# A GRU and an expert-choice FFN on one core: the loads and masks of the kernel's head are dealt out anew over three queues

## The chip, the cores and the metric

The kernel runs on 1 core of a Trainium2 chip. The time is device microseconds of one execution, the median of several; the profile is one further execution, recorded by the hardware profiler. A core has TensorE (PE; its weight loads are PEld), VectorE (DVE), ScalarE (ACT), GpSimd (POOL) and SyncE (SP). SP, ScalarE and GpSimd can each issue transfers (DMA), which 16 DMA engines carry out.

## The reference

```python
x: (16, 256, 512)   cond_2048: (16, 512)   # float32
# GRU over 256 steps, state h: (16, 512), first state cond_2048
gi = x_t @ W_ih + b_ih;  gh = h @ W_hh + b_hh          # 3 gates of 512 each
r = sigmoid(i_r + h_r);  z = sigmoid(i_z + h_z);  n = tanh(i_n + r * h_n)
h = (1 - z) * n + z * h                                 # the states are xf: (4096, 512)
# FFN: each of 16 experts takes its 256 best rows
S = softmax(xf @ router_w + router_b);  G, idx = top_k(S.T, 256)
y = zeros.at[idx].add(G[..., None] * (xf[idx] @ expert_w + expert_b))
out = x + y
```

All 16 experts share one matrix `expert_w`, so each row's product is the same for every expert that takes it.

## The kernel before, in words

Everything is float32 and stays in the core's memory: W_ih as `wih` and W_hh as `whh` (3 MB each, laid out as 128 partitions x 4 blocks x 3 gates x 512), x as `xs` (32 groups of 8 steps, 128 partitions x 512 each) and the states as `ht`. The 256 steps run one after the other. Step s adds h times `whh` into PSUM (`h_part`, L409, gates r, n, z in this order), ScalarE and VectorE make the new state from that (L465 to L505), and the next step needs it. The products of x with `wih` (`x_part`, L396) are made for two steps at a time and fill TensorE between. For that, a group of x is also loaded in another layout (`xa`, eight pieces of 32 KB, `load_xa`, L236) and turned by VectorE (`turn_x`, L252). `xa` has one buffer, which group 1 takes over after group 0.

Behind the steps follow the choice of the rows (a binary search over the scores), the expert's products that are still missing, and the output. The 0/1 matrices `ident`, `same_f`, `same_h`, `before_f` and `row_of` are used there alone, and are made at the very start by GpSimd and VectorE (L86 to L106) with scratch tiles in a pool of their own, `masks`. That pool is closed again before the weights' tiles are opened, so `wih` and its neighbours get the same room.

The head of the kernel, up to step 0, is what the change touches:
- GpSimd's queue: `zero` (L86, which TensorE's first operations read), the masks' operations, `c0` set to zero (L208), then four loads of biases (L266) and four of cond (L268).
- SP's and ScalarE's queues, each half of every weight load: wih's gate r, the eight pieces of x's group 0 (four each), wih's gates n and z, whh's gates r, n and z (`load_rows`, L228). SP goes on with group 1's `xa`, `expert_w`, `router_w` and two biases (L281 to L285).
- TensorE: PSUM cleared (L112), the biases added by matmuls (L300), then `x_part` for steps 0 to 3 (gates r and n first, then z), then step 0.
- VectorE: the masks' operations, x's group 0 turned, cond turned (L314), the biases copied out of PSUM (L309 to L311), the first state `hs` (L319), then step 0.

The order within SP's and ScalarE's queues of the head is written out by hand (`manual_schedule`, L272); for the others a scheduler sets the order there. In the recurrence it is written out for all engines. Loads from SP and ScalarE share eight semaphores in turn, and so do those from GpSimd with eight others: a load that takes over a semaphore waits in its queue until the load that had it has landed. Biases and cond are loaded into rooms of `xs` (groups 26 to 31) that x fills much later: `load_x` (L245) loads four pieces of group g during the steps of group g.

Of the kernel before, what the change touches and what calls it, by code (L numbers as in the profile page):

```python
# [8 lines left out]
F32 = mybir.dt.float32  # L9
BF16 = mybir.dt.bfloat16  # L10
F16 = mybir.dt.float16
I32 = mybir.dt.int32
# [6 lines left out]
def kernel(  # L19
# [34 lines left out]
    nc = tc.nc  # L54
    B, T, D = x.shape
    E = router_w.shape[1]
    P = 128
    QD = 32
    KC = D // P
    TG = P // B  # L60
    NG = T // TG
# [4 lines left out]
    xs = const.tile([P, NG, D], F32, name="xs")  # L66
# [11 lines left out]
    GH = P // E  # L78
    ident = const.tile([P, P], F32, name="ident")
# [4 lines left out]
    ones_b = const.tile([P, B], F32, name="ones_b")  # L84
    zero = const.tile([P, QD], BF16, name="zero")
    nc.gpsimd.memset(zero, 0.0)  # L86
    make_identity(nc, ident)
    nc.gpsimd.memset(ones_b, 1.0)
    with tc.tile_pool(name="masks", bufs=1) as mk:
        shift = GH.bit_length() - 1  # L90
        at = mk.tile([P, 3], I32, name="at")
        nc.gpsimd.iota(at[:, 0:1], pattern=[[0, 1]], base=0, channel_multiplier=1)
        nc.vector.tensor_single_scalar(at[:, 1:2], at[:, 0:1], shift, ALU.logical_shift_right)
        nc.vector.tensor_single_scalar(at[:, 2:3], at[:, 0:1], GH - 1, ALU.bitwise_and)
        at_f = mk.tile([P, 3], F32, name="at_f")
        nc.vector.tensor_copy(at_f, at)
        to_i = mk.tile([P, 2, E, GH], I32, name="to_i")
        nc.gpsimd.iota(to_i[:, 0, :, :], pattern=[[1, E], [0, GH]], base=0, channel_multiplier=0)
        nc.gpsimd.iota(to_i[:, 1, :, :], pattern=[[0, E], [1, GH]], base=0, channel_multiplier=0)
        to = mk.tile([P, 2, P], F32, name="to")  # L100
        nc.vector.tensor_copy(to, to_i.rearrange("p o e h -> p o (e h)"))
        nc.vector.tensor_scalar(same_f, to[:, 0, :], at_f[:, 1:2], None, ALU.is_equal)
        nc.vector.tensor_copy(same_h, same_f)
        nc.vector.tensor_scalar(before_f, to[:, 1, :], at_f[:, 2:3], None, ALU.is_gt)
        nc.vector.tensor_tensor(before_f, before_f, same_f, ALU.mult)
        nc.vector.tensor_scalar(row_of, to[:, 1, 0:GH], at_f[:, 2:3], None, ALU.is_equal)  # L106
# [77 lines left out]
    with (  # L184
# [17 lines left out]
        b_raw = xs[0:2, NG - 4 : NG - 1, :]  # L202
        b_n = xs[0:1, NG - 1, :]
        b_r = xs[0:1, NG - 6, 0:E]
        c0 = xs[:, NG - 5, 0:P]
        ones = wts.tile([2, QD], F32, name="ones")
        nc.vector.memset(ones, 1.0)
        nc.gpsimd.memset(c0, 0.0)  # L208

# [7 lines left out]
        def columns(ap, j):  # L219

            return ap.rearrange("p (c j i) -> p j c i", j=KC, i=QD)[:, j]

        def load_rows(dst, src, form):

            rows = src.rearrange(form, c=KC)
            for h in range(2):
                ks = slice(KC // 2 * h, KC // 2 * (h + 1))
                queues[h].dma_start(out=dst[:, ks, :], in_=rows[:, ks, :])  # L228
# [3 lines left out]
        def load_xa(g, xa, j, qs):  # L232

            for o in range(2):
                q = QD * j + B * o
                qs[o].dma_start(  # L236
                    out=xa[q : q + B],
                    in_=x[:, g * TG + o : (g + 1) * TG : 2, j * P : (j + 1) * P],
                )
# [7 lines left out]
        def new_xa():  # L247
            return xap.tile([P, TG // 2, P], F32, name="xa")

        def turn_x(g, xa):  # L250
            t = xtp.tile([P, TG // 2, P], F32, name="xt")
            nc.vector.transpose(  # L252
                t.rearrange("p q (c r) -> p q c r", c=KC), xa.rearrange("p q (i c) -> p q c i", c=KC)
            )
            xT[g] = t

        queues = (nc.sync, nc.scalar)
        ET = mybir.EngineType
        xa0 = new_xa()
        for dst, src in (  # L260
            (b_raw[0:1], b_ih.rearrange("(o g d) -> o g d", o=1, d=D)),
            (b_raw[1:2], b_hh.rearrange("(o g d) -> o g d", o=1, d=D)),
            (b_n, b_hh[2 * D :].rearrange("(o d) -> o d", o=1)),
            (b_r, router_b.rearrange("(o e) -> o e", o=1)),
        ):
            nc.gpsimd.dma_start(out=dst, in_=src)  # L266
        for j in range(KC):
            nc.gpsimd.dma_start(  # L268
                out=c0[QD * j : QD * j + B, :].rearrange("b (c i) -> b c i", c=KC), in_=columns(cond, j)
            )  # L270
        xa1 = new_xa()
        with tc.manual_schedule(engines={ET.SP, ET.Activation}):  # L272
            for i, gate in enumerate((0, 2, 1)):
                load_rows(wih[:, :, i, :], w_ih[:, gate * D : (gate + 1) * D], "(p c) n -> p c n")
                if i == 0:
                    for j in range(KC):
                        load_xa(0, xa0, j, queues)
            for gate in (0, 2, 1):
                load_rows(whh[:, :, gate, :], w_hh[:, gate * D : (gate + 1) * D], "(c p) n -> p c n")
            for j in range(KC):  # L280
                load_xa(1, xa1, j, (nc.sync, nc.sync))  # L281
            nc.sync.dma_start(out=ewr[:, :, E:], in_=expert_w.rearrange("(c p) n -> p c n", c=KC))
            nc.sync.dma_start(out=ewr[:, :, 0:E], in_=router_w.rearrange("(c p) n -> p c n", c=KC))
            nc.sync.dma_start(out=eb, in_=expert_b.rearrange("(o d) -> o d", o=1).to_broadcast([P, D]))
            nc.sync.dma_start(out=rb, in_=router_b.rearrange("(o e) -> o e", o=1).to_broadcast([P, E]))  # L285
# [131 lines left out]
                    )  # L417

        turn_x(0, xa0)
        xa_next = xa1  # L420
        for z in (False, True):
            for p in range(2):
# [10 lines left out]
        with tc.manual_schedule(engines={ET.PE, ET.Activation, ET.DVE, ET.Pool, ET.SP}):  # L433
            units = []
            for s in range(T):
                p, odd = divmod(s, 2)
                g, c = divmod(s, TG)
# [21 lines left out]
                elif not apart:  # L459
# [12 lines left out]
                t, n, nT, zT = (  # L472
                    [gp.tile([P, P // 2], F32, name=f"{name}{half}") for half in range(2)]
                    for name in ("t", "n", "nT", "zT")
                )
# [50 lines left out]
                elif g + 2 < NG:  # L526
                    if c == KC:
                        xa_next = new_xa()
                    j = c - KC
# [33 lines left out]
    with (  # L563
# [32 lines left out]
        for bit in range(HIGH, -1, -1):  # L596
# [6 lines left out]
            n = counts[:, bit : bit + 1]  # L603
# [63 lines left out]
        for g in [g for g in range(NG) if g not in late_groups] + late_groups:  # L667
            while g in late_groups and g not in late_done:
# [5 lines left out]
                out=out[:, g * TG : (g + 1) * TG, :], in_=xs[:, g, :]  # L674
# [32 lines left out]
```

## Time and profile before

| | |
|---|---|
| runs | 1201.14, 1201.27, 1209.14 us; median 1201.27 |
| the profiled execution | 1205.67 us, span from first to last instruction 1203.9 |
| TensorE busy | 1163.5 us, 97% of the span; weight loads 1052.9 us |
| VectorE, ScalarE, GpSimd busy | 699.1, 323.3, 96.0 us |
| mean granted clock of TensorE | 0.994 |
| GpSimd's last mask operation (L99) | starts at 1.66, takes 0.35 us |
| VectorE's mask operations (L93 to L106) | from 1.24 to 3.33 us |
| first weight load issued (SP and ScalarE, L228) | 3.42 us |
| x of group 0 turned (L252) | starts at 11.81, takes 1.08 us |
| first state (L319) | 13.73 us |
| stretch 40 to 1130 us (the steps) | TensorE busy 1076.7 of 1090 us, clock 1.00, 19 GB/s |

Times in the profile are microseconds from the span's start. Busy shares are tenths of a slice. A bracket behind an instruction says how long its engine sat idle before it, and what ended that idle time. The lists of loads give the number, the size of each and the median time from issue to landing. q1 and q10 are the queues of SP and ScalarE, q0 that of GpSimd.

### The profile page before, as it was taken

What the parts mean: (1) busy time and instruction counts of PE and PEld (TensorE: products, weight loads), DVE (VectorE), ACT (ScalarE), POOL (GpSimd) and SP (SyncE); (2) the same over time, 40 slices, a digit from 0 to 9 for tenths busy, and PEclk for the clock granted to TensorE, in tenths of its full rate; (3) what the DMA queues carried; (4) which work ended last, traced back from release to release, by engine and by line L of the source; (5) the groups of instructions that cost most, each with busy time, mean ns of one, the idle gap of its engine ahead of it and who ended that gap; (6) DMA issues with size and microseconds to landing.
All of it is one profiled execution on the core that took longest, in us unless ns stands there. A gap on an engine that the chain in (4) does not pass through costs nothing. (4 is left out here: it accounts for less than half of the span.)

```text
span 1203.9 us, 80849 instructions
## 1 busy us (share of the span) xinstructions
PE 1163.5 (97%) x36490; PEld 1052.9 (87%) x36490; DVE 699.1 (58%) x3919; ACT 323.3 (27%) x1435; POOL 96.0 (8%) x398
## 2 busy tenths in 40 slices
PE   5999999999999999999999999999999999999897
PEld 3899999999999999989999999999999999998443
DVE  2555655565555655555565555565565556565776
ACT  0222222222222222322222222222222222222220
POOL 2000000000000000000000000000000000000000
PEclk9999999999999999999999999999999999999998
DMA  7200000000000000000000000000000000000008
GB/s 233 63 22 20 20 19 21 19 20 19 20 22 20 19 18 22 20 20 17 22 19 20 19 21 20 20 19 20 22 18 21 18 22 20 20 9 13 2 2 281
DMA packets 48730, 38.06 MB, mean 32 GB/s; under 512 B 7744, under 2 KB 40576, under 8 KB 48384
## 3 DMA queue, kind: packets, MB, share of 16 engines
q1 hardware_dynamic: 46176, 29.56, 8.4%
q8 instruction: 286, 4.69, 1.6%
q10 hardware_dynamic: 1952, 3.28, 0.8%
q14 instruction: 60, 0.49, 0.1%
q0 software_dynamic: 256, 0.05, 0.0%
HBM read 24.47 MB, written 8.39 MB: 27 GB/s over the span
## 5 line engine op out<-in xcount | busy, mean ns | idle before, releaser
L409 PE MATMUL ra<-whh,hs 128*16 128x128 f32 (+1 forms) x8192 | 348.4, 274 | 6.9 <-DVE zT L494 4.9
L409 PE MATMUL hn<-whh,hs 128*16 128x128 f32 (+1 forms) x8192 | 348.1, 273 | 0.8 <-DMA whh<-in_L_cond_W_hh_dram 0.8
L482 DVE TENSOR_TENSOR t<-r,hn 128x64 f32<-128x64 f32 x512 | 90.2, 217 | 369.8 <-PE hn L409 366.8
L396 PE MATMUL ra<-wih,xt 128*32 128x256 f32 x4096 | 288.4, 381 | 5.1 <-DMA wih<-in_L_cond_W_ih_dram 3.2
L409 PE MATMUL zz<-whh,hs 128*16 128x128 f32 (+1 forms) x8192 | 288.2, 273 | 3.0 <-DMA whh<-in_L_cond_W_hh_dram 1.9
L409 PEld LDWEIGHTS hn<-whh,hs 128*16 128x16 f32 (+1 forms) x8192 | 259.7, 104 | 1.2 <-DMA whh<-in_L_cond_W_hh_dram 1.1
L409 PEld LDWEIGHTS ra<-whh,hs 128*16 128x16 f32 (+1 forms) x8192 | 246.3, 103 | 15.5 <-issue 5.9
L409 PEld LDWEIGHTS zz<-whh,hs 128*16 128x16 f32 (+1 forms) x8192 | 240.5, 103 | 6.4 <-issue 3.5
L465 ACT ACTIVATE r<-ra 128x128 f32<-128x128 f32 x256 | 71.1, 278 | 591.3 <-PE ra L409 591.3
L396 PEld LDWEIGHTS ra<-wih,xt 128*32 128x32 f32 x4096 | 158.9, 110 | 38.3 <-issue 11.6
L486 ACT ACTIVATE n<-t 128x64 f32<-128x64 f32 x512 | 103.5, 248 | 192.8 <-DVE t L484 192.6
L396 PE MATMUL zz<-wih,xt 128*32 128x128 f32 x4096 | 146.6, 273 | 1.9 <-issue 1.4
L396 PEld LDWEIGHTS zz<-wih,xt 128*32 128x32 f32 x4096 | 129.0, 110 | 17.1 <-issue 5.0
L491 DVE STREAM_TRANSPOSE nT<-n 128x64 f32<-128x64 f32 x512 | 100.6, 234 | 57.3 <-ACT n L486 57.0
L494 DVE STREAM_TRANSPOSE zT<-zs 128x64 f32<-128x64 f32 x512 | 121.8, 238 | 3.6 <-ACT zs L487 3.0
L505 DVE TENSOR_TENSOR hs<-v,nT 128x32 f32<-128x32 f32 x512 | 101.9, 199 | 21.7
L502 DVE TENSOR_TENSOR v<-u,zT 128x32 f32<-128x32 f32 x512 | 104.4, 204 | 8.9
L363 PE MATMUL pe<-ewr,ht 128*32 128x136 f32 (+1 forms) x1920 | 108.2, 276 | 0.0
L484 DVE TENSOR_TENSOR t<-t,ra 128x64 f32<-128x64 f32 x512 | 88.2, 213 | 0.1
L363 PEld LDWEIGHTS pe<-ewr,ht 128*32 128x32 f32 x1920 | 76.5, 110 | 10.9 <-issue 0.5
L497 DVE TENSOR_TENSOR u<-hs,nT 128x32 f32<-128x32 f32 x512 | 78.3, 153 | 0.0
L136 PE MATMUL pe<-ewr,ht 128*32 128x256 f32 x1088 | 69.5, 395 | 1.9 <-ACT pe L156 1.9
(107 smaller groups left out, 513.6 us busy)
## 6 DMA issues: line engine op xcount, KB each, us to landing
xs<-in_x_dram SPq DMA_DIRECT2D x128, 64.0 KB, 2.3
out_dram<-xs SPq DMA_DIRECT2D x32, 256.0 KB, 3.9
xa<-in_x_dram SPq DMA_DIRECT2D x252, 32.0 KB, 2.2
wih<-in_L_cond_W_ih_dram SPq DMA_DIRECT2D x3, 512.0 KB, 5.5
wih<-in_L_cond_W_ih_dram ACTq DMA_DIRECT2D x3, 512.0 KB, 6.2
whh<-in_L_cond_W_hh_dram SPq DMA_DIRECT2D x3, 512.0 KB, 11.6
whh<-in_L_cond_W_hh_dram ACTq DMA_DIRECT2D x3, 512.0 KB, 11.2
ewr<-in_L_ffn_expert_w_dram SPq DMA_DIRECT2D x1, 1024.0 KB, 5.3
```

What stands on the lines that cost most here:

```text
L363: nc.tensor.matmul(pe[quadrant(j), at : at + w], ht[:, g, k, quadrant(j)], ewr[:, k, src : src + w], start=(k == 0), stop=(k == KC - 1), t ...
L396: nc.tensor.matmul(dst, lhs, rhs, start=False, stop=(k == KC - 1), tile_position=(0, QD * j), skip_group_check=True)
L409: nc.tensor.matmul(dst[quadrant(j, m)], lhs, columns(whh[:, k, gate_, :], j), start=False, stop=(k == KC - 1), tile_position=(0, QD * j), ...
L465: nc.scalar.activation(r, ra[p % 2][:, 0, :], AF.Sigmoid)
L482: nc.vector.tensor_tensor(t[half], r[:, cols], hn[p % 2][:, cols], ALU.mult)
L484: nc.vector.tensor_tensor(t[half], t[half], ra[p % 2][:, 1, cols], ALU.add)
L486: nc.scalar.activation(n[half], t[half], AF.Tanh)
L491: nc.vector.transpose(nT[half], n[half])
L494: nc.vector.transpose(zT[half], zs[:, halves[half][1]])
L497: nc.vector.tensor_tensor(u[half], hs[:, halves[half][2], slot(s), :], of_step(nT[half], odd), ALU.subtract)
L502: nc.vector.tensor_tensor(v[half], u[half], of_step(zT[half], odd), ALU.mult)
L505: nc.vector.tensor_tensor(hs[:, halves[half][2], slot(s + 1), :], v[half], of_step(nT[half], odd), ALU.add)
```

## The change

Three things are done together. The masks are made in a function that is called behind `turn_x(0, xa0)`, with their scratch in groups 22 to 25 of `xs` in place of the pool `masks`. Group 0's `xa` is loaded by GpSimd's queue behind the biases, and cond behind it; SP and ScalarE start with the twelve weight loads in the order they had. The head's order on GpSimd's queue is now written out by hand too.

```diff
     nc.gpsimd.memset(zero, 0.0)
-    make_identity(nc, ident)
-    nc.gpsimd.memset(ones_b, 1.0)
-    with tc.tile_pool(name="masks", bufs=1) as mk:
+    def make_masks():
+        make_identity(nc, ident)
+        nc.gpsimd.memset(ones_b, 1.0)
         shift = GH.bit_length() - 1
-        at = mk.tile([P, 3], I32, name="at")
+        at = xs[:, NG - 7, 0:3].bitcast(I32)
...
-        at_f = mk.tile([P, 3], F32, name="at_f")
+        at_f = xs[:, NG - 8, 0:3]
...
-        to_i = mk.tile([P, 2, E, GH], I32, name="to_i")
+        to_i = xs[:, NG - 9, 0 : 2 * P].bitcast(I32).rearrange("p (o e h) -> p o e h", o=2, h=GH)
...
-        to = mk.tile([P, 2, P], F32, name="to")
+        to = xs[:, NG - 10, 0 : 2 * P].rearrange("p (o n) -> p o n", o=2)
...
-        nc.gpsimd.memset(c0, 0.0)
...
         xa0 = new_xa()
-        for dst, src in (... four biases ...):
-            nc.gpsimd.dma_start(out=dst, in_=src)
-        for j in range(KC):
-            nc.gpsimd.dma_start(out=c0[...], in_=columns(cond, j))
         xa1 = new_xa()
-        with tc.manual_schedule(engines={ET.SP, ET.Activation}):
+        with tc.manual_schedule(engines={ET.SP, ET.Activation, ET.Pool}):
             for i, gate in enumerate((0, 2, 1)):
                 load_rows(wih[:, :, i, :], w_ih[:, gate * D : (gate + 1) * D], "(p c) n -> p c n")
-                if i == 0:
-                    for j in range(KC):
-                        load_xa(0, xa0, j, queues)
             for gate in (0, 2, 1):
                 load_rows(whh[:, :, gate, :], w_hh[:, gate * D : (gate + 1) * D], "(c p) n -> p c n")
+            for dst, src in (... four biases ...):
+                nc.gpsimd.dma_start(out=dst, in_=src)
+            for j in range(KC):
+                load_xa(0, xa0, j, (nc.gpsimd, nc.gpsimd))
+            nc.gpsimd.memset(c0, 0.0)
+            for j in range(KC):
+                nc.gpsimd.dma_start(out=c0[...], in_=columns(cond, j))
             for j in range(KC):
                 load_xa(1, xa1, j, (nc.sync, nc.sync))
...
         turn_x(0, xa0)
+        make_masks()
```

In the order of instructions that comes out, TensorE's is the same as before. GpSimd's head is: `zero`, four biases, four pieces of x, four more that each wait for one of the biases to land, `c0` and `ident` set, cond's four loads that each wait for one of x's first four pieces, then the rest of the masks. VectorE's is: the biases' copies, x turned, cond turned, the first state, the nine mask operations, step 0. The first eight weight loads wait for nothing, the last four for the first four.

More of the change, by code (lines that the diff above doesn't have):

```diff
@@ L259 @@
         xa0 = new_xa()
[L260 to L265, printed above, removed]
-            nc.gpsimd.dma_start(out=dst, in_=src)
-        for j in range(KC):
-            nc.gpsimd.dma_start(
-                out=c0[QD * j : QD * j + B, :].rearrange("b (c i) -> b c i", c=KC), in_=columns(cond, j)
-            )
         xa1 = new_xa()
-        with tc.manual_schedule(engines={ET.SP, ET.Activation}):
+        with tc.manual_schedule(engines={ET.SP, ET.Activation, ET.Pool}):
             for i, gate in enumerate((0, 2, 1)):
                 load_rows(wih[:, :, i, :], w_ih[:, gate * D : (gate + 1) * D], "(p c) n -> p c n")
-                if i == 0:
-                    for j in range(KC):
-                        load_xa(0, xa0, j, queues)
             for gate in (0, 2, 1):
                 load_rows(whh[:, :, gate, :], w_hh[:, gate * D : (gate + 1) * D], "(c p) n -> p c n")
+            for dst, src in (
+                (b_raw[0:1], b_ih.rearrange("(o g d) -> o g d", o=1, d=D)),
+                (b_raw[1:2], b_hh.rearrange("(o g d) -> o g d", o=1, d=D)),
+                (b_n, b_hh[2 * D :].rearrange("(o d) -> o d", o=1)),
+                (b_r, router_b.rearrange("(o e) -> o e", o=1)),
+            ):
+                nc.gpsimd.dma_start(out=dst, in_=src)
[3 more added lines that the diff above has]
+            for j in range(KC):
+                nc.gpsimd.dma_start(
+                    out=c0[QD * j : QD * j + B, :].rearrange("b (c i) -> b c i", c=KC), in_=columns(cond, j)
+                )
             for j in range(KC):
```

## The prediction

> **What bounds the kernel now.** I read the page first (which engine is full, and where), then the time line of the first 43 us, then the waits of SP's and TensorE's queues there, then the DMA view in stretches of 1 to 3 us.
>
> The page, busy shares in 40 slices of 30.1 us each:
> ```profile
> PE   5999999999999999999999999999999999999897
> PEld 3899999999999999989999999999999999998443
> DMA  7200000000000000000000000000000000000008
> ```
> TensorE is busy from the second slice on, and DMA is loaded only at the two ends. The diff touches only what runs ahead of the recurrence, and TensorE's order is the same instruction by instruction. So the change can act in the first slice alone: its result is how much earlier or later the chain of 256 steps starts.
>
> The time line of TensorE, from the first x-parts to step 1 (start us, duration, engine, line):
> ```profile
> 15.29 5.21 PE L396 MATMUL ra<-wih,xt 128*32 128x256 f32 x64 [3.23 <-DMA wih<-in_L_cond_W_ih_dram]
> ...
> 22.05 0.62 PE L409 MATMUL ra<-whh,hs 128*16 128x128 f32 x16
> 23.48 0.63 PE L409 MATMUL hn<-whh,hs 128*16 128x128 f32 x16 [0.81 <-DMA whh<-in_L_cond_W_hh_dram]
> ...
> 26.85 1.07 PE L409 MATMUL zz<-whh,hs 128*16 128x128 f32 x32 [1.86 <-DMA whh<-in_L_cond_W_hh_dram]
> ```
> The x-parts (L396) start at 15.29 when the second gate of wih is in. Their last weight load is followed by the first one of step 0 (L409) at 21.95, so they last 6.66. Step 0 then waits twice for whh. Step 1's first weight load is at 29.11, step 2's at 34.66, step 3's at 38.73, step 4's at 42.85. A step at its pace is thus 4.1 (38.73 less 34.66 is 4.07; 42.85 less 38.73 is 4.12). Step 0 lasts 7.16, which is 3.05 too long; step 1 lasts 5.55, which is 1.45 too long.
>
> Why step 1 is long (columns: stretch, its length, busy us of PE, PEld, DVE, ACT, POOL, granted clock, DMA share, GB/s):
> ```profile
> 6.00:9.00 3.00, 0.26 (x8) 0.00 (x0) 0.00 (x0) 0.00 (x0) 0.25 (x1) 1.00 1.02 348
> 9.00:12.00 3.00, 2.51 (x56) 1.95 (x56) 0.19 (x1) 0.00 (x0) 0.00 (x0) 1.00 0.48 105
> 12.00:15.00 3.00, 0.06 (x4) 0.00 (x0) 1.90 (x6) 0.00 (x0) 0.18 (x1) 1.00 1.04 388
> ...
> 27.00:30.00 3.00, 1.78 (x50) 1.50 (x45) 1.20 (x7) 0.28 (x1) 0.17 (x1) 0.79 0.26 53
> 30.00:33.00 3.00, 3.00 (x78) 3.00 (x73) 0.34 (x3) 0.28 (x1) 0.00 (x0) 0.65 1.05 357
> ```
> After the waits for whh the granted clock falls to 0.79 and 0.65; that is the 1.45. The first three rows show a second thing: DMA is full at 6 to 9 and from 12, and moves 105 GB/s between them, although 5 MB of weights are still to come. SP's queue says why, and why it starts late:
> ```profile
> SPq L236 <- DMA wih<-in_L_cond_W_ih_dram: 3.2, 1, 3.2
> SPq L228 <- DVE row_of L106: 2.7, 1, 2.7
> SPq L228 <- DMA xa<-in_x_dram: 1.4, 3, 0.7
> ```
> The first weight load waits 2.7 us for the last mask operation, whose room the weights reuse. Then x's pieces and the next weights wait for earlier loads to land, because a load waits for the one eight places ahead of it.
>
> **The change, part by part.**
>
> Removed: the 2.7 wait. SP and ScalarE issue their first weights at about 0.72 instead of 3.42, and eight of the twelve without any wait. Weights then flow without the hole. Size: 12 loads of 0.524 MB are 6.29 MB, at 388 GB/s 16.2 us. Before, the 3 us row ending at 6.0 had moved 0.24 MB (0.6 us at full rate), so the equivalent start is 5.4, 2.0 after the issue; now 2.7. x of the head is 0.26 MB in 512-byte rows, about 1.1 us at the 244 GB/s of the stretch from 8 to 9 us. Sum: 2.7 + 16.2 + 1.1 + 0.2 for biases and cond = 20.2; plus 1.0 for the stragglers, the last whh is in at 21.2. The first two gates of wih (2.1 MB, 5.4 us) are in at about 9.
>
> Moved: x's eight pieces, to GpSimd, behind four biases. This is what decides. What a landing on that queue costs, in the stretch from 4 to 6 us, beside SP's and ScalarE's own (q0, GpSimd's queue: packets, MB, share; then loads: number, KB each, median us from issue to landing):
> ```profile
> q0 software_dynamic: 53, 0.01, 2.3%
> ...
> xa<-in_x_dram SPq DMA_DIRECT2D x3, 32.0 KB, 5.7
> xa<-in_x_dram ACTq DMA_DIRECT2D x3, 32.0 KB, 5.9
> xs<-in_cond_dram POOLq DMA_DIRECT2D x4, 8.0 KB, 5.8
> xs<-in_L_ffn_router_b_dram POOLq DMA_DIRECT2D x1, 0.1 KB, 5.7
> ```
> Ahead of the weights the first three biases took 1.7 to 2.3; beside them a 0.1 KB load took 5.7. From 6 to 7 us that queue (q0) moved not one packet, with 193 of the others. So a landing costs 1.7 at least, 5.6 to 6.0 where weights flow, and at most until the weights are through. I take 5.7 to 5.8, the rows with weights in flight; both ends stay for the range.
>
> GpSimd, from its rows: zero ends at 0.86; b_ih's issue takes 0.65, three more 0.49 each: issued at 0.88, 1.53, 2.02, 2.51. x's pieces 1 to 4, 0.52 each (price of cond's issue): 2.99 to 5.07. Pieces 5 to 8 reuse the biases' semaphores: each waits for one bias to land. The last waits for router_b: 2.51 + 5.7 = 8.2; it lands at 8.2 + 5.8 = 14.0. Turning x (L252) takes 1.08: the x-parts start at 15.1, against 15.29 before. That is the odd result: x goes from early to last, and the early weights wait for it.
>
> Queued behind these waits on GpSimd: cond's four loads, which also wait for x's pieces 1 to 4 (landing 8.8 to 10.4), so issued by 10.9 and landed by 16.7; then the identity, ones and three iotas (0.29 + 0.11 + 0.13 + 0.28 + 0.35, about 1.2): 12.1. On VectorE: bias copies (biases at 8.2, then about 2.9 of L300 on TensorE, hidden before 15.1), x, cond, hs at about 17.3, then nine mask operations of 2.08 in all, by 19.5. Step 0's first VectorE operation comes some 2.3 after the x-parts' end at 21.75, at 24: 4.5 spare. If cond landed 4.5 later, the masks would cost directly. SP's other loads: x of group 1 now waits for x turned (15.1, before 12.9), but stood behind whh until 18.86 anyway; it is needed at 43.6. Masks in x's room: groups 22 to 25 are loaded from step 176 on, some 730 us later: nothing.
>
> Sum: x-parts 0.2 earlier; step 0 without its whh waits 3.05 less (z's part needs whh at 21.75 + 1.8 = 23.5, it is in at 21.2); step 1 at full clock 1.45 less. Total 4.7 less. It is taken on one execution of 1205.67 (span 1203.9 and 1.8 around it), 4.4 above the runs' median of 1201.27; I subtract from the median: **1196.6**.
>
> One rule is set beside this. The Trainium skill, "DMA: Bandwidth & Descriptors" (Anatomy of one DMA, SWDGE path), gives a load from GpSimd 2.0 us plus bytes over 436 GB/s, by estimate 2.1 for a piece of x; the trace agrees ahead of the weights (1.7 to 2.3) and not beside them (5.7). With 2.1 the sum would be that of the first rival, 1194.2. The same page (Issuing engine by pattern) gives simple loads to Sync as the generally faster path, which speaks against this change; the rows beside weights show no difference between the three queues (5.7, 5.9, 5.8).
>
> **The rivals.** With L the time of a landing on GpSimd's queue, two rounds of it (a bias, then a piece of x) stand before the x-parts, so the result is -4.7 + 2 (L - 5.75).
>
> Fast queue: L is 2.3, the dearest bias before the weights. Pieces issue back to back from 2.99, the last at 6.6, land at 8.9; turned at 10.0; x-parts end at 16.7. Now whh bounds: 21.2 for its last gate, and step 1 follows 2.26 later as before (29.11 less 26.85): 23.5. Gain 5.6, and 1.45 if the clock holds: 1194.2. For it: all engines are quiet when the biases go out. Against: all four biases now go out after the first weights, not before.
>
> Even: with weights queued three and four deep, L grows to about 8; gain 4.7 less 4.5 to 4.7: about 1201.2. For it: the waits grew with what was ahead (xa of group 1 landed 8.5 after its issue behind whh). Against: those were on SP's own queue, behind its own weights.
>
> Slower, by starving: GpSimd's queue is served only when the weights have passed. For it: no q0 packet from 5.4 to 7.6, and the rush at 8 to 9, when the first weights were through. Against: cond's four loads each took 5.6 to 5.9, not ever less as the end neared. Then weights end at 18.9, biases land at 19.9, pieces 5 to 8 issue at 19.9 to 22.0, land at 23.8, turned at 24.9; x-parts end at 31.5, step 1 at 35.6, 6.5 later than before, less 1.45: 5.1 more, 1206.4. It decides once L is over 8.1.
>
> **How the numbers follow.** Likeliest (L 5.4 to 6.5: 1195.4 to 1198.1) 0.42; fast queue 0.18; even 0.2; starving 0.2. Leaving out the starving case alone would already use up the 2 in 10 that may be missed, with nothing left for the sizes, so the range runs from half a microsecond under the fast queue, 1193.7, to the starving, 1206.4. One per cent is 12 us, about what a measurement of this kernel can tell; no case comes near, so within 1% has 0.97, faster 0.01, slower 0.02, for something I have not seen.
>
> **What would show it.** Right: first weights issued under 1 us; DMA near 390 GB/s with no hole from 4 to 19 us; x's last piece issued near 8 and turned near 14; no wait for whh in step 0; clock 1.00 in step 1; step 1 at about 25.9. Wrong: x turned after 19, biases landing after 12, VectorE's masks between hs and step 0 in the chain, or any difference behind 60 us.

## The result, and the profile after

The changed kernel took 1204.43 us (median of 12 runs, 1199.16 to 1207.28), the one before 1203.91 (12 runs; the three runs shown above lay at the low end). The two medians differ by 0.5 us to the worse. The ratio over all runs is 0.9994, with a 95% interval of 0.9976 to 1.0012, which is 0.7 us to the better: not to be told from no change. Forecast were 4.7 us less. That the median lies inside the forecast range says little, as the range is 12.7 us wide; the gain does not show.

The profiled execution of the changed kernel took 1206.33 us, its span is 1204.3. Its head, in TensorE's time line (start us, duration; L396 and L409 of the kernel before are now L398 and L411):
```profile
18.14 5.82 PE L398 MATMUL ra<-wih,xt 128*32 128x256 f32 x64 [5.96 <-DVE xt L253]
...
25.53 0.61 PE L411 MATMUL ra<-whh,hs 128*16 128x128 f32 x16
...
29.63 0.64 PE L411 MATMUL ra<-whh,hs 128*32 128x128 f32 x16 [1.30 <-DVE zT L497]
...
33.71 0.63 PE L411 MATMUL ra<-whh,hs 128*16 128x128 f32 x16 [1.25 <-DVE hs L508]
```
The x-parts are no longer released by wih but by x turned on VectorE, and start at 18.14 in place of 15.29. Step 0 has no wait for whh left. In numbers (the x-parts by their first matmul, the steps by their first weight load):

| us | before | after | forecast |
|---|---|---|---|
| x-parts start | 15.29 | 18.14 | 15.1 |
| step 0 | 21.95 | 25.43 | 21.75 |
| step 1 | 29.11 | 29.60 | 25.9 |
| step 2 | 34.66 | 33.71 | 30.0 |

So the chain of steps starts 0.95 earlier and not 4.7. What came in between is on GpSimd's queue:
```profile
1.34 0.64 POOL L274 DMA_DIRECT2D xs<-in_L_cond_b_ih_dram  x1 [0.47 <-issue]
1.97 0.97 POOL L274 DMA_DIRECT2D xs<-in_L_cond_b_hh_dram  x2
2.93 0.48 POOL L274 DMA_DIRECT2D xs<-in_L_ffn_router_b_dram  x1
3.41 2.06 POOL L237 DMA_DIRECT2D xa<-in_x_dram  x4
7.22 0.51 POOL L237 DMA_DIRECT2D xa<-in_x_dram  x1 [1.76 <-DMA xs<-in_L_cond_b_ih_dram]
8.48 1.54 POOL L237 DMA_DIRECT2D xa<-in_x_dram  x3 [0.74 <-DMA xs<-in_L_cond_b_hh_dram]
```
Four pieces of x go out at once, then GpSimd stands still until a bias has landed. The last piece is issued at 9.50 (the third of the three from 8.48). The loads issued from 8.4 to 9 and from 10 to 10.5, where this last piece is the only one of x:
```profile
xa<-in_x_dram POOLq DMA_DIRECT2D x2, 32.0 KB, 5.9
...
whh<-in_L_cond_W_hh_dram ACTq DMA_DIRECT2D x1, 512.0 KB, 13.7
xa<-in_x_dram POOLq DMA_DIRECT2D x1, 32.0 KB, 7.2
```
So the last piece was in at 16.7, and VectorE turned x at 17.00. The three pieces ahead of it took 5.9 each. The list of loads of the same execution (number, KB each, median us from issue to landing):
```profile
xa<-in_x_dram POOLq DMA_DIRECT2D x8, 32.0 KB, 6.3
xs<-in_cond_dram POOLq DMA_DIRECT2D x4, 8.0 KB, 6.4
xs<-in_L_cond_b_ih_dram POOLq DMA_DIRECT2D x1, 6.0 KB, 5.6
xs<-in_L_cond_b_hh_dram POOLq DMA_DIRECT2D x1, 6.0 KB, 6.2
xs<-in_L_cond_b_hh_dram POOLq DMA_DIRECT2D x1, 2.0 KB, 6.2
xs<-in_L_ffn_router_b_dram POOLq DMA_DIRECT2D x1, 0.1 KB, 6.3
```
All four biases now cost about what only router_b cost before (5.7). And in stretches of 3 us (busy us of PE, PEld, DVE, ACT, POOL, then granted clock, DMA share, GB/s):
```profile
3.00:6.00 3.00, 0.00 (x0) 0.00 (x0) 0.00 (x0) 0.00 (x0) 2.46 (x5) 1.00 1.02 386
6.00:9.00 3.00, 0.67 (x16) 0.70 (x20) 0.00 (x0) 0.00 (x0) 1.03 (x3) 1.00 1.07 358
9.00:12.00 3.00, 3.00 (x72) 2.72 (x64) 0.65 (x2) 1.28 (x1) 2.79 (x7) 1.00 1.05 324
12.00:15.00 3.00, 0.18 (x4) 0.00 (x0) 0.38 (x2) 0.00 (x0) 1.58 (x7) 1.00 1.07 304
...
30.00:33.00 3.00, 2.46 (x92) 2.19 (x81) 1.13 (x9) 0.99 (x5) 0.00 (x0) 1.00 0.27 71
```
The hole of 105 GB/s is gone and the clock is full in step 1, both as forecast. But the flow falls to 324 and 304 while x's pieces move, and the last load of whh, issued at 10.16, lands at 23.8 (13.7 later, in the lines above), not at the 21.2 of the forecast. It held nothing, as x was later still.

### The profile page after: what moved, and what is told of

The parts are those of the page before. It is cut to its first block, busy times and chain, and to the rows that moved or that the text cites. A ratio compares the mean times of both kernels' runs of the same rounds, so it can differ in the third digit from the quotient of the medians.

```text
span 1204.3 us, 80850 instructions
## 1 busy us (share of the span) xinstructions
PE 1162.3 (97%) x36490; PEld 1048.4 (87%) x36490; DVE 699.2 (58%) x3919; ACT 323.3 (27%) x1435; POOL 100.2 (8%) x406
## 5 line engine op out<-in xcount | busy, mean ns | idle before, releaser
L411 PE MATMUL ra<-whh,hs 128*16 128x128 f32 (+1 forms) x8192 | 345.6, 273 | 7.6 <-DVE zT L497 5.2
L411 PE MATMUL hn<-whh,hs 128*16 128x128 f32 (+1 forms) x8192 | 345.4, 273 | 0.0
L398 PE MATMUL ra<-wih,xt 128*32 128x256 f32 x4096 | 288.0, 382 | 7.6 <-DVE xt L253 6.0
L411 PE MATMUL zz<-whh,hs 128*16 128x128 f32 (+1 forms) x8192 | 287.8, 273 | 2.6 <-issue 2.4
L411 PEld LDWEIGHTS ra<-whh,hs 128*16 128x16 f32 (+1 forms) x8192 | 243.3, 103 | 16.8 <-issue 6.8
L411 PEld LDWEIGHTS hn<-whh,hs 128*16 128x16 f32 (+1 forms) x8192 | 256.8, 103 | 0.4 <-issue 0.2
L411 PEld LDWEIGHTS zz<-whh,hs 128*16 128x16 f32 (+1 forms) x8192 | 239.6, 103 | 6.2 <-issue 5.5
L398 PEld LDWEIGHTS ra<-wih,xt 128*32 128x32 f32 x4096 | 156.6, 111 | 43.2 <-issue 8.3
L398 PE MATMUL zz<-wih,xt 128*32 128x128 f32 x4096 | 147.1, 273 | 1.5 <-issue 1.2
L398 PEld LDWEIGHTS zz<-wih,xt 128*32 128x32 f32 x4096 | 128.9, 110 | 17.2 <-issue 4.1
```

What stands on the lines that cost most here:

```text
L398: nc.tensor.matmul(dst, lhs, rhs, start=False, stop=(k == KC - 1), tile_position=(0, QD * j), skip_group_check=True)
L411: nc.tensor.matmul(dst[quadrant(j, m)], lhs, columns(whh[:, k, gate_, :], j), start=False, stop=(k == KC - 1), tile_position=(0, QD * j), ...
```

## The experiments

Two theories were set against each other. **Two rounds**: the x-parts wait for two landings in series on GpSimd's queue (a bias, then a piece of x), each dear because weights are in flight. **Flow**: the weights themselves hold the x-parts, wherever x is loaded. Two rivals more: GpSimd's queue is slow by amount and not by rounds; and the steps give back what the head gains. All kernels start from the changed one unless said otherwise. Of each kernel one execution was profiled, and e1 to e5 ran only that once: they are read from the head alone. The mark "group 1" is VectorE's turn of x's group 1 in step 3: 43.59 before, 42.63 after.

**x back at SP and ScalarE (e1).**
```diff
 load_rows(wih[:, :, i, :], ...)
+if i == 0:
+    for j in range(KC):
+        load_xa(0, xa0, j, queues)
...
-for j in range(KC):
-    load_xa(0, xa0, j, (nc.gpsimd, nc.gpsimd))
```


> x's eight pieces go back to SP and ScalarE behind the first gate of wih; masks stay late, so only the early start of the weights is left of the change. Theory (two rounds of landings on GpSimd's queue hold the x-parts, not the weights): the head is that of before, 2.67 us earlier: x turned at about 9.1, x-parts at 12.6, the waits for whh and the slow clock in step 1 come back, step 1 at 26.4, step 2 at 32.0 (before 34.66, after 33.71). Rival (the flow of the weights holds the x-parts, wherever x is loaded): x-parts not before 17, step 2 at 33.7 or later.

Measured: x turned at 9.82, x-parts at 11.62, a little earlier than the 12.6 expected. TensorE's time line of this kernel:
```profile
18.25 0.63 PE L412 MATMUL ra<-whh,hs 128*16 128x128 f32 x16
20.87 0.88 PE L412 MATMUL hn<-whh,hs 128*16 128x128 f32 x16 [1.99 <-DMA whh<-in_L_cond_W_hh_dram]
...
23.86 1.37 PE L412 MATMUL zz<-whh,hs 128*16 128x128 f32 x32 [0.40 <-DMA whh<-in_L_cond_W_hh_dram]
26.45 0.65 PE L412 MATMUL ra<-whh,hs 128*32 128x128 f32 x16 [1.23 <-DVE zT L498]
```
Step 1 is at 26.45, about 2.7 earlier than before: the masks' 2.7 in full, and 3.2 earlier than with x at GpSimd. Here the waits for whh set the head again; its last load landed at 24.5, before at 27.2. The theory of flow is out for the x-parts. Step 2 came at 30.53 and not at 32.0: the slow clock fell into step 0, behind the first wait (0.52 from 21 to 24), and was gone in step 1. Group 1 at 40.21.

**x split over three queues (e2).**
```diff
+if i == 0:
+    for j in range(KC // 2, KC):
+        load_xa(0, xa0, j, queues)
...
-for j in range(KC):
+for j in range(KC // 2):
     load_xa(0, xa0, j, (nc.gpsimd, nc.gpsimd))
```


> Four of x's eight pieces by SP and ScalarE behind the first gate of wih, four by GpSimd behind the biases: no piece waits for a bias to land. Theory (two rounds): the last of GpSimd's four pieces is issued at 5.0 and lands 6.3 to 7.5 later, at 11.3 to 12.5; x-parts at 12.4 to 13.6, ended by 20.5; then the last gate of whh holds step 0, landing at about 23, step 1 at 25.3, step 2 at 29.4 (30.9 if the clock falls). Rival (flow of weights): x-parts at 17 or later, step 2 at 33.7.

Measured, from this kernel's time line:
```profile
12.21 0.29 DVE L315 COPY bias<-zz 128x128 f32<-128x128 f32 x1 [0.17 <-PE zz L305]
12.60 1.08 DVE L253 STREAM_TRANSPOSE xt<-xa 128x512 f32<-128x512 f32 x1
13.74 6.33 PE L401 MATMUL ra<-wih,xt 128*32 128x256 f32 x64 [1.62 <-DVE xt L253]
...
25.74 0.65 PE L414 MATMUL ra<-whh,hs 128*32 128x128 f32 x16 [1.28 <-DVE zT L500]
...
32.19 0.51 PE L414 MATMUL hn<-whh,hs 128*16 128x128 f32 x10 [0.67 <-issue]
```
No piece waits for a bias, and x is turned 4.4 earlier than after although four pieces still go by GpSimd (7.0 each). The last of them was in at 11.7; what x's turn then stood behind is the copying of the biases, the first line, which comes first in VectorE's order. Step 1 at 25.74 and step 2 at 29.82 are near the 25.3 and 29.4 of the theory of two rounds, but in part by luck: the last gate of whh, which was to hold step 0, held nothing, and in its place the x-parts lasted 7.8. New is the last line: in step 2 TensorE stops for something that the profile does not show, and step 3 starts at 34.94, 1.0 late. Group 1 at 39.76.

**The other half alone (e3)**: the kernel before, with x's pieces at GpSimd behind the biases; the masks stay first, in their own room.

> The other half of the change alone: x's pieces by GpSimd behind the biases, but the masks first and in their own room as before, so the weights start at 3.42. Theory (two rounds on GpSimd's queue): biases from 2.10, the last lands at 10.0, x's last piece issued at 10.1 and landed by 17.5; x-parts at 18.6, only 0.5 later than after; step 2 at 34.2 to 34.7. Rival (the weights' start sets the head): 2.67 later than after, step 2 at 36.4.

Measured:
```profile
9.88 0.51 POOL L236 DMA_DIRECT2D xa<-in_x_dram  x1 [2.12 <-DMA xs<-in_L_ffn_router_b_dram]
...
17.07 1.08 DVE L252 STREAM_TRANSPOSE xt<-xa 128x512 f32<-128x512 f32 x1 [4.47 <-DMA xs<-in_cond_dram]
18.18 8.62 SPq L236 DMA_DIRECT2D xa<-in_x_dram  x8
18.21 5.46 PE L395 MATMUL ra<-wih,xt 128*32 128x256 f32 x64 [6.00 <-DVE xt L252]
```
The weights start 2.67 later than after, and the x-parts at 18.21, the same as after (18.14). Step 2 is at 33.42 where the rival had 36.4. The first three biases go out ahead of the weights and land in 1.7 to 2.0, but the last piece of x waits for the fourth, router_b. That one is issued at 3.72 (after: 2.93) beside the weights, takes 5.9, and lets the piece out at 9.88 (after: 9.50); the piece takes 6.9 (after: 7.2). How early the weights start hardly enters this sum. So with x at GpSimd the early weights buy nothing in the head. (The profile puts VectorE's wait down to cond, here and after, because cond's loads use the same semaphores again. Cond's first load landed at 17.20, behind the turn's start; x's last piece at 16.8.)

**No bias loads (e4)**: the four loads are left out, with zeros in their place, so that x's pieces wait for nothing. This kernel leaves out the biases.

> As after, but the four biases are not loaded; zeros stand in their place (this part of the computation is left out). x's eight pieces then wait for nothing. Theory (two rounds, each piece landing some 6.3 to 7.5 after its issue, several under way together): last piece issued at 5.0, landed at 11.3 to 12.5, x-parts at 12.4 to 13.6; step 1 at 25.3 by the last gate of whh. Rival (GpSimd's queue moves so little beside the weights that the amount counts, not the rounds): eight pieces take as long as in after less the four small biases, x's last piece lands at 15 or later, x-parts at 16 or later.

Measured:
```profile
1.35 4.17 POOL L237 DMA_DIRECT2D xa<-in_x_dram  x8 [0.48 <-issue]
...
12.55 1.08 DVE L253 STREAM_TRANSPOSE xt<-xa 128x512 f32<-128x512 f32 x1 [5.76 <-DMA xa<-in_x_dram]
13.69 6.17 PE L393 MATMUL ra<-wih,xt 128*32 128x256 f32 x64 [7.28 <-DVE xt L253]
```
Eight pieces, 7.1 each (the median), all in by 12.55: they overlap. Not the amount counts but the second round. Step 1 at 25.52, near the 25.3 expected, but not by that way: as in e2 no wait for whh was left, and the x-parts lasted 7.6.

**x in front (e5).**
```diff
+for j in range(KC):
+    load_xa(0, xa0, j, queues)
 for i, gate in enumerate((0, 2, 1)):
     load_rows(wih[:, :, i, :], ...)
```
(and no pieces by GpSimd)

> x's eight pieces are issued by SP and ScalarE ahead of all weights; masks late, biases and cond by GpSimd. Theory (a small load is quick ahead of the weights and takes 6 us or more beside them, and the head goes by the last of x, biases and whh): x's pieces land by about 4.5, the weights start at about 2.5, biases land at 8.9 and their matmuls end at 12.5, x-parts at 12.5, whh's last gate lands at 21.7 to 23.2, step 1 at 24.0 to 25.5; group 1 turned (in step 3, 42.63 in after, 43.59 before) at 38.0 to 39.5. Rival (the start of the weights is what counts): 1.75 later than with x behind the first gate (40.21), 42.0.

Measured: group 1 at 41.08, a miss by 1.6, and nearer to the rival's 42.0 than to the theory's 39.5. GpSimd's loads of this kernel:
```profile
xs<-in_L_cond_b_ih_dram POOLq DMA_DIRECT2D x1, 6.0 KB, 2.2
xs<-in_L_cond_b_hh_dram POOLq DMA_DIRECT2D x1, 6.0 KB, 2.1
xs<-in_L_cond_b_hh_dram POOLq DMA_DIRECT2D x1, 2.0 KB, 2.2
xs<-in_L_ffn_router_b_dram POOLq DMA_DIRECT2D x1, 0.1 KB, 5.5
```
The biases are issued at the same times as after (1.33 to 2.93), but the weights at 2.58 in place of 0.75, and three of them land in a third of the time. That is the clearest test of the price: it is set by weights in flight. The x-parts start at 11.25, and then whh is the late one:
```profile
20.16 0.63 PE L411 MATMUL hn<-whh,hs 128*16 128x128 f32 x16 [1.50 <-DMA whh<-in_L_cond_W_hh_dram]
...
23.15 1.26 PE L411 MATMUL zz<-whh,hs 128*16 128x128 f32 x32 [1.49 <-DMA whh<-in_L_cond_W_hh_dram]
25.63 1.08 PE L411 MATMUL ra<-whh,hs 128*32 128x128 f32 x16 [1.22 <-DVE hs L508]
```
Step 1 starts at 25.63, hardly earlier than with x split, and lasts 6.53, at a clock that has fallen behind TensorE's two waits:
```profile
24.00:27.00 3.00, 1.78 (x44) 1.53 (x39) 1.20 (x7) 0.28 (x1) 0.17 (x1) 0.62 0.43 104
27.00:30.00 3.00, 3.00 (x64) 3.00 (x60) 0.60 (x4) 0.31 (x2) 0.00 (x0) 0.50 1.04 362
```
I had priced the waits for whh and left the clock out. That, and not the later start of the weights, is what brings group 1 near the rival's number: step 1 itself starts 0.8 earlier than with x behind the first gate (26.45), where the rival has it 1.75 later.

**The expert's loads at step 3 (e6, e7, e8)**, added to x in front, x split, and x back at SP and ScalarE:
```diff
-nc.sync.dma_start(out=ewr[:, :, E:], in_=expert_w...)   # and router_w, eb, rb
...
+if s == 3:
+    nc.sync.dma_start(out=ewr[:, :, E:], in_=expert_w...)   # and router_w, eb, rb
```


> As the run with x in front, and expert_w, router_w and two biases (1.3 MB) are issued at step 3 in place of behind the weights. Theory (TensorE's wait for nothing visible in step 2, 0.4 to 1.2 us in the kernels with an earlier head, is its next instructions, which are fetched beside that load): the wait is gone, group 1 is turned 13.0 after step 1's start as in after, at 37.0 to 38.5, 5 to 6.5 earlier than before; the time follows, ratio 0.995 to 0.996. Rivals: the wait belongs to the instruction stream and stays, 0.4 to 1.2 later than that; or the steps give an earlier head back, ratio 1.000.

> As the run with x split over three queues, and the expert's loads at step 3. Theory: group 1 turned at 38.8 in place of 39.76, ratio to before 0.996. Rivals: the wait in step 2 stays and group 1 is turned at 39.5 to 40; or the steps give an earlier head back, ratio 1.000.

> As the run with x back at SP and ScalarE behind the first gate, and the expert's loads at step 3. Theory: group 1 turned at 39.5 in place of 40.21, ratio 0.9966; so the masks' move alone is worth about three times what the whole change brought. Rivals: the wait in step 2 stays (40.2); or an earlier head is given back in the steps, ratio 1.000.

Measured, five rounds each beside the kernel before (median 1204.79 over its runs there; the line "after" is the result above, from other runs; step 1 of e6 to e8 by its first matmul, which is 0.03 behind the first weight load):

| kernel | step 1 | step 1 lasts | group 1, less before's | time, ratio to before |
|---|---|---|---|---|
| before | 29.11 | 5.55 | | 1 |
| after | 29.60 | 4.11 | -0.96 | 0.9994 (0.9976 to 1.0012) |
| e6 | 25.33 | 5.69 | -3.63 | 1201.50, 0.9972 (0.9955 to 0.9989) |
| e7 | 25.86 | 4.08 | -4.73 | 1200.27, 0.9967 (0.9949 to 0.9984) |
| e8 | 26.80 | 6.45 | -1.42 | 1203.65, 0.9988 (0.9971 to 1.0005) |

The wait in step 2 (0.4 in e1, 0.7 in e2, 0.2 in e3, 1.2 in e4) is in none of the three. But e5, with the load in its old place, did not have it either, and neither had the changed kernel: that it went with that load rests on one execution each of e7 and e8, and that it was for instructions is argued only. For e7 group 1 came out as expected, though in it too x's turn (13.46) stands behind the copies of the biases and not behind x. In its profile:
```profile
38.86 1.17 DVE L253 STREAM_TRANSPOSE xt<-xa 128x512 f32<-128x512 f32 x1 [0.18 <-issue]
```
e6 and e8 missed by 1.5 and 2.7: the waits for whh were there as in e5 and e1, and behind them the slow clock in step 1, in e8
```profile
24.00:27.00 3.00, 1.48 (x37) 1.03 (x41) 1.00 (x7) 0.28 (x1) 0.17 (x1) 0.67 0.11 31
27.00:30.00 3.00, 3.00 (x61) 3.00 (x57) 0.23 (x2) 0.28 (x1) 0.00 (x0) 0.50 0.17 47
```
e1 and e8 have nearly the same head up to here, and step 1 lasts 4.08 in one and 6.45 in the other. The ratios follow the head: 0.9967 is 4.0 less for a head 4.73 earlier, 0.9972 is 3.4 for 3.63, 0.9988 is 1.4 for 1.42, 0.9994 is 0.7 for 0.96. The intervals are about 2 us to either side, so only e6 and e7 are clear of no change, by 0.3%; for these two the rival that the steps give an earlier head back falls. That the early weights alone (e8) save time was expected at 0.9966 and is not shown.

Yet one profile cannot show such gains in its span. The changed kernel's 0.95 had turned into 0.4 more at the end. Group by group its lead was 0.96 at group 1, 0.30 at group 12, then 3.00 behind at group 14 and 1.13 behind at group 31. TensorE's waits from 415 to 490 us, after:
```profile
PE zz L411 <- issue: 2.4, 3, 1.1
PE ra L398 <- issue: 0.4, 1, 0.4
```
and in the kernel before, the same stretch:
```profile
PE ra L409 <- DVE zT L494: 0.2, 1, 0.2
```
These are stops without a visible cause like the one in e2, and the two executions have them at other places. That the runs of one kernel differ by up to 10 us through the like of them is likely and not shown. The prediction took any difference behind 60 us for a sign of being wrong; in a single execution these stops make such a difference, and no run ties them to the change. That is why the head is read from the profile's first 45 us, and the time from many runs.

## Why the prediction was wrong, point by point

- **Early weights: right in the start, not in the end.** First issue at 0.75 (forecast 0.72), eight without a wait, no hole. But the last of whh was in at 23.8 and not at 21.2. By the rows from 6 to 15 us, an estimate, the fallen flow (358, 324 and 304 for 388) is worth 1.4 of this; the rest is open. By the forecast's own times step 0's third part, due at 23.5, would have waited for it a little; x's delay hid this.
- **Which wait takes over: right.** x, moved behind two landings, sets the x-parts; VectorE's masks ended at 20.5 and cost nothing.
- **Step 0 without waits for whh, step 1 at full clock: right.** 4.17 and 4.11, forecast 4.1 each.
- **The failed step: "a landing costs ... I take 5.7 to 5.8".** The two rounds were as forecast, their price was not, and the x-parts came 3.04 later. 0.42 of it: GpSimd begins later (1.34, after a pause of 0.47 behind `zero`). 0.59: the first round (router_b) took 6.3, not 5.7. 0.28: from that landing at 9.22 to the last piece's issue, which the sum left out. 1.41: the last piece took 7.2, not 5.8. (The trace counts a landing in sixteen steps; fifteen of this one were done at 15.35, 5.85 after its issue, and the last came at 16.72.) 0.28: from its landing to the turn, left out too. Why the landings took longer is open. The row of 5.7 came from an execution with one gate in flight ahead of the loads, and now there were several; but the three pieces ahead of the last one took 5.9 beside the same gates, as forecast. The forecast's own formula, -4.7 + 2 (L - 5.75), gives -2.7 with the mean of 6.75, between the likeliest case and "even". (By this formula the likeliest case ends at 1195.9 and not at 1195.4.)
- **The x-parts' length: missed.** I kept 6.66; they took 7.29. TensorE took its weight loads at 0.43 for four until 22.41, which is 4.3 us at half pace against 3.0 before. The granted clock's column shows 1.00 all through this. The idle time ahead of them does not explain it: it was 5.96 here for a length of 7.29 and 3.23 before for 6.66, but 1.62 in e2 for 7.79 and 6.00 in e3 for 6.92. The cause stays open.
- **Sum**: 3.04 + 0.63 + 0.07 of steps 0 and 1 = 3.74; 4.7 less 3.74 is, but for rounding, the 0.95 that the profile shows.
- The rule on a load from GpSimd that the prediction weighed ("DMA: Bandwidth & Descriptors" of the Trainium skill, 2.1 by estimate) holds in e5 for the loads ahead of the weights (2.1 to 2.2) and in no run beside them (3.7 to 7.7).

## What to carry to other kernels

Before a small load is moved to another queue, look whether its semaphore makes it wait for an earlier load, and price every such round by the slowest landing seen beside the same traffic, not by one row with less in flight: the last piece decides. In the head, the early start of the weights was worth 2.7 us (e1) and was spent on a second round. Taking away that round (e7: four pieces per side, none of which waits for a bias) and moving a late-needed load out of the way gave 0.9967 (0.9949 to 0.9984). A wait ahead of TensorE can cost twice, its length and a slow clock behind it: in the kernel before, e5, e6 and e8 the step behind the waits for whh lasted 5.55 to 6.53 in place of 4.1.

## What the runs showed of the hardware that was not expected

- A bias of 0.1 to 6 KB took 1.7 to 2.3 us ahead of the weights and 5.4 to 7.4 beside them, on GpSimd's queue; x's 32 KB pieces show the same at ScalarE (2.2 in front, 5.7 behind the first gate). It is not one price per landing: in e1 cond's four loads, the last on that queue, took 4.8, 4.5, 4.2 and 3.9.
- While GpSimd's queue moved x, all queues together fell from about 388 GB/s to 304 to 324 (in e2 and e7 to 290 to 314), though x is only 0.26 MB.
- The price of a fallen clock is not fixed: step 1 lasted 4.08, 5.55, 5.69, 6.45 or 6.53 behind waits for whh in step 0. In the kernel with 4.08 (e1) the slow stretch fell into step 0. The Trainium skill, "TensorE: Matmul & The Clock Gate" (Part 1), says that the clock follows activity in a window of about 3.4 us that runs freely; that would let e1 and e8 differ as they do, but no run here shows the window itself.
